# The score product of a spiking recommender as two float32r passes, with the table fetched 14 chunks ahead and statistics in groups of two steps

## The chip, the cores and the metric

The kernel runs on one NeuronCore of a Trainium2 chip. The metric is device time in microseconds (us) of one execution; several runs give a median. Engines are called by their names: TensorE (PE in the profile, its weight loads PEld), VectorE (DVE), ScalarE (ACT), GpSimd (POOL) and SyncE (SP, which here only issues transfers). The 16 DMA engines of the core carry all transfers.

## What is computed

The inputs are a batch of 1,024 sequences of 50 item numbers, a length for each sequence, a table of 100,001 items with 128 float32 features, and gamma and beta of a batch normalisation. Cut to what matters:

```python
emb = emb_table.at[0].set(0.0)
prefix = jnp.cumsum(emb[seq], axis=1)
denom = jnp.minimum(t_idx[None, :], lengths[:, None])
uF = prefix / denom[:, :, None]
y = (uF - uF.mean(axis=0)) * rsqrt(uF.var(axis=0) + 1e-5) * gamma + beta
# for each of the 50 steps: v += (x - v) / 2; spike = v >= 1; v -= spike
rate = spikes.mean(axis=0)          # 1024 x 128
scores = rate @ emb.T               # 1024 x 100001
```

The scores alone are 409.6 MB in float32, and the table is 51.2 MB.

## The kernel before

There are two stages, and features lie on the 128 partitions in both.

**First stage, the steps (lines 59 to 149).** For each of the 50 time steps, GpSimd issues eight indirect gathers (line 105), 128 rows of the table each, into a buffer `e` of which there are six. ScalarE clears a buffer before its gathers (line 103). TensorE transposes the eight blocks into a PSUM tile `eT` (line 115). VectorE adds it to the running prefix `pre` (line 116), divides by the lengths into `uF` (117) and takes batch statistics (120, 121). Five steps form a group (TG = 5): only when the statistics of all five stand are the short operations on mean and variance done (124 to 136). Then ScalarE normalises each step into `xh` (141, 143), and VectorE runs the neuron: `v`, `negv` and `count` (146 to 148), three passes over 128x1024 a step. At the end `rateT`, the count divided by 50, is the stationary side of the score product (149).

**Second stage, the scores (lines 163 to 203).** The table is taken in 49 chunks of 2,048 items, the last one shorter. A chunk is fetched by a transfer of 1 MB that ScalarE issues, into one of three `rows` buffers (166 to 173). TensorE transposes it, in 16 blocks, into two PSUM tiles `pt` of 1,024 columns (183). VectorE and ScalarE in turn copy them to `embT` (186, by the helper of lines 155 to 161). For each of eight blocks of 128 sequences TensorE multiplies: four products of 512 columns, into two PSUM tiles `po` of 1,024 columns (195). VectorE evicts the first and ScalarE the second into an output tile `o` (202), and SyncE issues the store of 1 MB (203). There are eight `o` buffers and four PSUM tiles, shared by `eT`, `pt` and `po`.

A scheduler sets the order of the instructions on each engine from the program, and may move an instruction of the second stage ahead of late ones of the first. Each engine then works through its list in that order, and waits at an instruction until all that it needs is there.

Of the kernel before, what the change touches and what calls it, by code (L numbers as in the profile page):

```python
# [12 lines left out]
F32 = mybir.dt.float32  # L13
I32 = mybir.dt.int32
# [14 lines left out]
def rec_kernel(  # L29
# [19 lines left out]
    rowp = ctx.enter_context(tc.tile_pool(name="rows", bufs=3))  # L49
    embp = ctx.enter_context(tc.tile_pool(name="embT", bufs=2))  # L50
# [4 lines left out]
    # rateT[d, b]: the mean of the spikes over time, the stationary side of the score product.  # L55
    rateT = const.tile([P, B], F32, tag="rateT", name="rateT")

    # ---------------- prefix means, batch norm and spikes: D on partitions, batch on columns
    with ExitStack() as ph:
# [6 lines left out]
        # Item 0 has a zero embedding: its index goes out of bounds, where the gather leaves the  # L66
        # zeros that the tile was cleared to.
# [8 lines left out]
        # 1 / min(t, length) = max(1 / t, 1 / length)  # L76
# [9 lines left out]
        # x / tau with tau = 2: half of gamma and beta.  # L86
# [8 lines left out]
        nc.vector.memset(count, 0.0)  # L95

        for g in range(T // TG):
# [25 lines left out]
            # rsqrt(var + eps): a square root, its reciprocal, and one Newton step on that.  # L123
# [14 lines left out]
            for j in range(TG):  # L138
# [5 lines left out]
                # v <- v + (x - v) / 2; spike = v >= V_TH; v <- v - spike, kept negated.  # L144
# [10 lines left out]
    def evacuate(dst, src):  # L155
        nonlocal turn
        if turn % 2 == 0:
            nc.vector.tensor_copy(dst, src)  # L158
        else:
            nc.scalar.copy(dst, src)  # L160
        turn += 1

    for c0 in range(0, N, CH):
        w = min(CH, N - c0)
        full, rest = divmod(w, P)
        rows = rowp.tile([P, CH // P, D], F32, tag="rows", name=f"rows_{c0}")
        if full:
            nc.scalar.dma_start(
                out=rows[:, :full, :],
                in_=table[c0 : c0 + full * P, :].rearrange("(k p) d -> p k d", p=P),  # L170
            )
# [51 lines left out]
```

## Time and profile before

| | |
|---|---|
| median of 3 runs | 2107.3 us (2107.03 to 2107.64) |
| the profiled execution: its span, first to last instruction | 2106.9 us |
| TensorE busy, matmuls | 1627.1 us, 77% |
| VectorE busy | 912.5 us, 43% |
| ScalarE busy | 609.2 us, 29% |
| GpSimd busy | 457.0 us, 22% |
| HBM written, read | 409.60 MB, 78.15 MB |

The profile is of one execution, and its span is what there is of that execution's own time; it stands 0.4 us under the median. Shares of the span are averages over two stages that work differently, so a reader should go by stretches: the first stage ends at the first product of the scores, 640.28 us after the start, and the second takes the rest. Busy time of a matmul is counted from its start to its modelled end, and neighbours overlap; how far apart they follow each other is read from a run of many, divided by their number.

### The profile page before, as it was taken

The page shows a single profiled execution, that of the slowest core. Times are in us where ns is not written, and L with a number is a line of the kernel's source. Part 1 is how long each engine was busy: PE and PEld are TensorE (multiplying, and loading weights), DVE is VectorE, ACT ScalarE, POOL GpSimd, SP SyncE. Part 2 cuts the span into 40 slices and gives each one's busy share as a digit, 9 for nine tenths or more (in the row PEclk, how much of TensorE's full clock was granted, in tenths as well). Part 3 has the DMA queues.
Part 4 walks back from the last instruction along what each step waited for, and adds up shares of the span by engine and source line. Part 5 has one row for each costly group of instructions (what it writes and reads, how often), then busy time and mean ns, then how long its engine had stood idle before and what let it go on. Part 6 is the DMA issues. An engine that isn't in the chain of part 4 may idle for free.

```text
span 2106.9 us, 13798 instructions
## 1 busy us (share of the span) xinstructions
PE 1627.1 (77%) x4318; PEld 754.1 (36%) x4318; DVE 912.5 (43%) x921; ACT 609.2 (29%) x651; POOL 457.0 (22%) x406
## 2 busy tenths in 40 slices
PE   2333233333318999999999999999999999999998
PEld 1111111111103444444444444444444444444444
DVE  4443766557574333333333333333333333333333
ACT  2212323323132323333333323332333333323332
POOL 6777777777700000000000000000000000000000
PEclk9999999999999999999999999999999999999999
DMA  4111111111105888887888788888887888788867
GB/s 116 48 45 47 43 46 46 46 45 44 44 25 222 313 320 317 317 311 315 319 319 312 315 317 316 316 316 317 317 316 310 317 319 319 309 316 317 313 277 292
DMA packets 97862, 488.69 MB, mean 232 GB/s; under 512 B 14811, under 2 KB 16508, under 8 KB 48636
## 3 DMA queue, kind: packets, MB, share of 16 engines
q1 hardware_dynamic: 57920, 410.36, 48.6%
q10 hardware_dynamic: 27068, 51.20, 8.2%
q0 software_dynamic: 12800, 26.24, 4.7%
q8 instruction: 34, 0.56, 0.1%
q14 instruction: 40, 0.33, 0.0%
HBM read 78.15 MB, written 409.60 MB: 232 GB/s over the span
## 4 chain that ended last, share of the span: by engine, by line
PE 66%; issue 14%; POOL 13%; DVE 5%; DMA 1%; POOLq 0%; ACT 0%; ACTq 0%
PE po L195 64%; POOL e L105 13%; DVE embT L158 3%; PE pt L183 2%; DMA e<-in_L_rec_emb_table,idx 1%; DVE v L146 1%; DVE negv L147 1%; POOLq L105 0%; DVE bs L120 0%; DVE uF L117 0%; DVE pre L116 0%; DVE count L148 0%; ACT xh L143 0%; ACT uF L141 0%; POOLq L219 0%
## 5 line engine op out<-in xcount | busy, mean ns | idle before, releaser
L195 PE MATMUL po<-embT,rateT 128*128 128x512 f32 x3136 | 1356.1, 593 | 71.0 <-DVE rateT L149 49.5
L195 PEld LDWEIGHTS po<-embT,rateT 128*128 128x128 f32 x3136 | 591.8, 190 | 807.0 <-issue 655.9
L158 DVE COPY o<-po 128x1024 f32<-128x1024 f32 x392 | 480.0, 1224 | 859.8 <-PE po L195 859.8
L160 ACT COPY o<-po 128x1024 f32<-128x1024 f32 (+1 forms) x392 | 394.4, 1006 | 995.3 <-PE po L195 995.3
L115 PE MATMUL eT<-ident,e 128*128 128x128 f32 x400 | 183.6, 469 | 402.2 <-DMA e<-in_L_rec_emb_table,idx 355.5
L105 POOL DMA_INDIRECT e<-in_L_rec_emb_table,idx x400 | 456.3, 1141 | 126.1 <-issue 114.9
L115 PEld LDWEIGHTS eT<-ident,e 128*128 128x128 f32 x400 | 72.5, 184 | 513.0 <-DMA e<-in_L_rec_emb_table,idx 399.9
L103 ACT ACTIVATE e<-e 128x1024 uint32<-128x1024 uint32 x50 | 52.3, 1055 | 368.2 <-PE eT L115 263.2
L158 DVE COPY embT<-pt 128x1024 f32<-128x1024 f32 x49 | 60.0, 1225 | 93.5 <-PE pt L183 93.5
L183 PEld LDWEIGHTS pt<-ident,rows 128*128 128x128 f32 x782 | 90.0, 142 | 27.2 <-issue 25.5
L183 PE MATMUL pt<-ident,rows 128*128 128x128 f32 x782 | 95.4, 276 | 1.3 <-DVE embT L158 1.3
L116 DVE TENSOR_TENSOR pre<-pre,eT 128x1024 f32<-128x1024 f32 x50 | 59.7, 1195 | 65.6 <-issue 39.6
L146 DVE SCALAR_TENSOR_TENSOR v<-negv,xh 128x1024 f32<-128x1024 f32 x50 | 61.1, 1221 | 55.5 <-issue 40.2
L143 ACT ACTIVATE xh<-uF,hgb,a 128x1024 f32<-128x1024 f32 x50 | 59.9, 1228 | 62.2 <-DVE a L134 32.3
L120 DVE BATCH_NORM_STATS2 bs<-uF 128x6 f32<-128x512 f32 x100 | 66.5, 685 | 0.5
L117 DVE SCALAR_TENSOR_TENSOR uF<-rlen,pre 128x1024 f32<-128x1024 f32 x50 | 61.0, 1219 | 0.4
L148 DVE SCALAR_TENSOR_TENSOR count<-v,count 128x1024 f32<-128x1024 f32 x50 | 61.0, 1219 | 0.0
L147 DVE SCALAR_TENSOR_TENSOR negv<-v 128x1024 f32<-128x1024 f32 x50 | 60.7, 1214 | 0.2
L160 ACT COPY embT<-pt 128x1024 f32<-128x1024 f32 (+1 forms) x49 | 49.3, 1006 | 33.0 <-PE pt L183 33.0
L141 ACT ACTIVATE uF<-uF,nm 128x1024 f32<-128x1024 f32 x50 | 53.2, 1133 | 0.0
L128 DVE RECIPROCAL r<-r 128x5 f32<-128x5 f32 x10 | 1.9, 189 | 110.3 <-issue 80.8
L127 ACT ACTIVATE r<-ve 128x5 f32<-128x5 f32 x10 | 2.0, 196 | 33.7 <-DVE ve L125 33.7
(26 smaller groups left out, 37.1 us busy)
## 6 DMA issues: line engine op xcount, KB each, us to landing
scores<-o SPq DMA_DIRECT2D x384, 1024.0 KB, 3.9
scores<-o SPq DMA_DIRECT2D x8, 848.5 KB, 3.5
e<-in_L_rec_emb_table,idx POOLq DMA_INDIRECT x400
rows<-in_L_rec_emb_table ACTq DMA_DIRECT2D x1, 832.0 KB, 7.2
rows<-in_L_rec_emb_table ACTq DMA_DIRECT2D x48, 0.5 KB, 7.7
len_i<-in_r_lengths SPq DMA_DIRECT2D x1, 512.0 KB, 5.2
seq_sb<-in_r_seq SPq DMA_DIRECT2D x1, 200.0 KB, 2.9
rows<-in_L_rec_emb_table ACTq DMA_DIRECT2D x1, 16.5 KB
```

Source lines behind the costliest of these rows:

```text
L105: nc.gpsimd.indirect_dma_start(out=e[:, n * P : (n + 1) * P], out_offset=None, in_=table, in_offset=bass.IndirectOffsetOnAxis(ap=idx[:, n, ...
L115: nc.tensor.transpose(eT[:, n * P : (n + 1) * P], e[:, n * P : (n + 1) * P], ident)
L117: nc.vector.scalar_tensor_tensor(uF[:, j, :], rlen, 1.0 / (t + 1), pre, ALU.max, ALU.mult)
L120: nc.vector.bn_stats(bs[:, h, :], uF[:, j, h * BANK : (h + 1) * BANK])
L143: nc.scalar.activation(xh, x, AF.Identity, bias=hgb[:, 1:2], scale=a[:, j : j + 1])
L146: nc.vector.scalar_tensor_tensor(v, negv, -0.5, xh, ALU.mult, ALU.add)
L147: nc.vector.scalar_tensor_tensor(negv, v, V_TH, v, ALU.is_ge, ALU.subtract)
L148: nc.vector.scalar_tensor_tensor(count, v, V_TH, count, ALU.is_ge, ALU.add)
L158: nc.vector.tensor_copy(dst, src)
L160: nc.scalar.copy(dst, src)
L183: nc.tensor.transpose(pt[:, k0 : k0 + kw], rows[:kw, (h0 + k0) // P, :], ident[:kw, :kw])
L195: nc.tensor.matmul(po[:, k0 : k0 + kw], lhsT=rateT[:, n * P : (n + 1) * P], rhs=embT[:, h0 + k0 : h0 + k0 + kw], start=True, stop=True,)
```

## The change

1. **The score product.** `rateT` gives way to `countR`, the integer counts themselves, in the type float32r. Each half of a chunk leaves PSUM in two parts: `hi`, which ScalarE writes as float32r, and `lo`, the difference between the PSUM tile and `hi`, which VectorE computes and writes as float32r. Each float32 product of 512 columns becomes two float32r products that add up in PSUM, one with `hi` and one with `lo`. The division by 50 is done at the eviction, as a multiplication by VectorE and ScalarE in turn.
2. **The table.** There are 14 `rows` buffers instead of three. The fetches go out from SyncE instead of ScalarE: 14 ahead of the first step, and each further one when the transposes of a chunk are through, in SyncE's list between the stores of two chunks.
3. **The steps.** TG = 2: the statistics are finished for two steps together, in 25 groups instead of 10.
4. **The buffers.** There are four `o` buffers instead of eight.

```diff
-TG = 5  # time steps whose batch statistics are finished together
+TG = 2
+AHEAD = 14
...
-    rowp = ctx.enter_context(tc.tile_pool(name="rows", bufs=3))
-    embp = ctx.enter_context(tc.tile_pool(name="embT", bufs=2))
+    rowp = ctx.enter_context(tc.tile_pool(name="rows", bufs=AHEAD))
...
-    rateT = const.tile([P, B], F32, tag="rateT", name="rateT")
+    countR = const.tile([P, B], F32R, tag="countR", name="countR")
+    held = {}
+    def fetch(c0):
+        w = min(CH, N - c0)
+        full, rest = divmod(w, P)
+        rows = rowp.tile([P, CH // P, D], F32, tag="rows", name=f"rows_{c0}")
+        if full:
+            nc.sync.dma_start(
+                out=rows[:, :full, :],
+                in_=table[c0 : c0 + full * P, :].rearrange("(k p) d -> p k d", p=P),
+            )
...
+        held[c0] = rows
+    def rows_of(c0):
+        if c0 + AHEAD * CH < N:
+            todo.append(c0 + AHEAD * CH)
+        return held.pop(c0)
...
+        for c0 in range(0, min(AHEAD * CH, N), CH):
+            fetch(c0)
 
         for g in range(T // TG):
...
-        nc.vector.tensor_scalar_mul(rateT, count, 1.0 / T)
-    op = ctx.enter_context(tc.tile_pool(name="o", bufs=8))
+        nc.vector.tensor_copy(countR, count)
+    op = ctx.enter_context(tc.tile_pool(name="o", bufs=4))
+    embp = ctx.enter_context(tc.tile_pool(name="embT", bufs=2))
...
-            nc.scalar.dma_start(
-                out=rows[:, :full, :],
...
+        rows = rows_of(c0)
+        hi = embp.tile([P, CH], F32R, tag="hi", name=f"hi_{c0}")
+        lo = embp.tile([P, CH], F32R, tag="lo", name=f"lo_{c0}")
...
-            evacuate(embT[:, h0 : h0 + hw], pt[:, :hw])
+            nc.scalar.copy(hi[:, h0 : h0 + hw], pt[:, :hw])
+            nc.vector.tensor_tensor(
+                lo[:, h0 : h0 + hw], pt[:, :hw], hi[:, h0 : h0 + hw].bitcast(F32), ALU.subtract
+            )
+        while todo:
+            fetch(todo.pop())
...
-                    nc.tensor.matmul(
-                        po[:, k0 : k0 + kw],
-                        lhsT=rateT[:, n * P : (n + 1) * P],
-                        rhs=embT[:, h0 + k0 : h0 + k0 + kw],
-                        start=True,
-                        stop=True,
-                    )
-                evacuate(o[:, h0 : h0 + hw], po[:, :hw])
+                    kw += kw % 2
+                    for part, first in ((hi, True), (lo, False)):
+                        nc.tensor.matmul(
+                            po[:, k0 : k0 + kw],
+                            lhsT=countR[:, n * P : (n + 1) * P],
+                            rhs=part[:, h0 + k0 : h0 + k0 + kw],
+                            start=first,
+                            stop=not first,
+                        )
+                if turn % 2 == 0:
+                    nc.vector.tensor_scalar_mul(o[:, h0 : h0 + hw], po[:, :hw], 1.0 / T)
+                else:
+                    nc.scalar.mul(o[:, h0 : h0 + hw], po[:, :hw], 1.0 / T)
+                turn += 1
```

The scheduler's order changes at three places that the prediction speaks of.

**VectorE, late in the first stage.** Before, this stood in VectorE's list (`embT` and `pt` are the first chunk's copy and its transposes; `eT`, `pre`, `uF` are of steps 46 and 47, counted from 0, and `v` is of step 40):

```order
L116 TENSOR_TENSOR pre<-pre,eT_2474 128x1024
L131 SCALAR_TENSOR_TENSOR q_2362<-q_2362,ve_2357 128x5
L121 BN_AGGR mv_2406<-bs_2444 128x2
L117 SCALAR_TENSOR_TENSOR uF_2405<-rlen,pre 128x1024
L132 SCALAR_TENSOR_TENSOR r_2359<-q_2362,r_2359 128x5
L158 COPY embT_2672<-pt_0_2673 128x1024
L134 TENSOR_SCALAR a_2366<-r_2359,hgb 128x5
L120 BN_STATS bs_2485<-uF_2405 128x6 x2
L116 TENSOR_TENSOR pre<-pre,eT_2515 128x1024
L146 SCALAR_TENSOR_TENSOR v_2373<-negv,xh_2371 128x1024
```

With the change the list ends the first stage so (`v_2900` and `v_2907` are the last two steps, `lo` is the first chunk's):

```order
L175 SCALAR_TENSOR_TENSOR v_2900<-negv,xh_2898 128x1024
L176 SCALAR_TENSOR_TENSOR negv<-v_2900 128x1024
L177 SCALAR_TENSOR_TENSOR count<-v_2900,count 128x1024
L175 SCALAR_TENSOR_TENSOR v_2907<-negv,xh_2905 128x1024
L205 TENSOR_TENSOR lo_2924<-pt_0_2925,hi_2923 128x1024
L176 SCALAR_TENSOR_TENSOR negv<-v_2907 128x1024
L177 SCALAR_TENSOR_TENSOR count<-v_2907,count 128x1024
L205 TENSOR_TENSOR lo_2924<-pt_1024_2936,hi_2923 128x1024
L178 CAST countR<-count 128x1024
L228 TENSOR_SCALAR o_0_2949<-po_0_0_2950 128x1024
```

The first chunk's copy out of `pt` stood ahead of the statistics of step 46, of steps 47 to 49, and of the neuron of steps 40 to 49; now its successor, the subtraction into `lo`, stands among the neuron's last passes. In TensorE's list the first chunk's transposes follow those of all 50 steps, before and now.

**SyncE, at the start.** Before, SyncE's list went on from the four small loads to the first store:

```order
L84 DMA gb<-in_L_rec_gamma 128x1
L85 DMA gb<-in_L_rec_beta 128x1
L203 DMA scores<-o_0_2693 128x2048
L203 DMA scores<-o_1_2703 128x2048
L203 DMA scores<-o_2_2713 128x2048
```

and now the 14 fetches stand between (the `rows` are those of chunks 0 to 13, of which five are shown):

```order
L110 DMA gb<-in_L_rec_gamma 128x1
L111 DMA gb<-in_L_rec_beta 128x1
L67 DMA rows_107<-in_L_rec_emb_table 128x16x128
L67 DMA rows_110<-in_L_rec_emb_table 128x16x128
L67 DMA rows_112<-in_L_rec_emb_table 128x16x128
L67 DMA rows_114<-in_L_rec_emb_table 128x16x128
L67 DMA rows_116<-in_L_rec_emb_table 128x16x128
```

The fetch of chunk 14 stands ahead of the first store, and each later one ahead of the first store of a chunk. In GpSimd's list nothing is moved: eight gathers for each step, and from the ninth on each waits for the landing of the gather eight places ahead of it.

**VectorE, between two chunks.** Now the list reads, from the sixth block of a chunk to the first of the next:

```order
L228 TENSOR_SCALAR o_5_3019<-po_5_0_3020 128x1024
L228 TENSOR_SCALAR o_6_3033<-po_6_0_3034 128x1024
L205 TENSOR_TENSOR lo_3062<-pt_0_3063,hi_3061 128x1024
L228 TENSOR_SCALAR o_7_3047<-po_7_0_3048 128x1024
L205 TENSOR_TENSOR lo_3062<-pt_1024_3074,hi_3061 128x1024
L228 TENSOR_SCALAR o_0_3087<-po_0_0_3088 128x1024
```

and before:

```order
L158 COPY o_5_2743<-po_5_0_2744 128x1024
L158 COPY o_6_2753<-po_6_0_2754 128x1024
L158 COPY o_7_2763<-po_7_0_2764 128x1024
L158 COPY embT_2775<-pt_0_2776 128x1024
L158 COPY o_0_2796<-po_0_0_2797 128x1024
```

The first half of the next chunk (`lo_3062<-pt_0`) is subtracted ahead of the eviction of the last block (`o_7`), where before the one copy stood behind it. TensorE's list holds, now as before, the 16 transposes of the next chunk behind the last product of this one.

## Rows read from the trace of the kernel before

**Rows 1.** The page, span in 40 equal slices: TensorE, GpSimd, DMA, busy tenths

```profile
PE   2333233333318999999999999999999999999998
...
POOL 6777777777700000000000000000000000000000
...
DMA  4111111111105888887888788888887888788867
```

**Rows 2.** The page, costliest groups: line, engine, operation; busy us, mean ns; idle

```profile
L195 PE MATMUL po<-embT,rateT 128*128 128x512 f32 x3136 | 1356.1, 593 | 71.0 <-DVE rateT L149 49.5
...
L158 DVE COPY o<-po 128x1024 f32<-128x1024 f32 x392 | 480.0, 1224 | 859.8 <-PE po L195 859.8
...
L160 ACT COPY o<-po 128x1024 f32<-128x1024 f32 (+1 forms) x392 | 394.4, 1006 | 995.3 <-PE po L195 995.3
...
L105 POOL DMA_INDIRECT e<-in_L_rec_emb_table,idx x400 | 456.3, 1141 | 126.1 <-issue 114.9
...
L146 DVE SCALAR_TENSOR_TENSOR v<-negv,xh 128x1024 f32<-128x1024 f32 x50 | 61.1, 1221 | 55.5 <-issue 40.2
...
L120 DVE BATCH_NORM_STATS2 bs<-uF 128x6 f32<-128x512 f32 x100 | 66.5, 685 | 0.5
```

**Rows 3.** Chain that ended last, one chunk: start us, us, what

```profile
670.79 1.24 DVE embT L158
...
672.07 27.73 PE po L195 x64
...
700.72 1.24 DVE embT L158
```

**Rows 4.** Busy time in four stretches: engines, granted clock, DMA share, GB/s

```profile
556.90:587.50 30.60, 12.09 (x30) 5.60 (x30) 0.03 (x1) 0.00 (x0) 20.71 (x21) 1.00 0.18 46
...
1000.00:1300.00 300.00, 295.56 (x808) 139.43 (x806) 110.96 (x91) 91.24 (x101) 0.00 (x0) 1.00 0.82 315
...
1001.00:1011.00 10.00, 9.76 (x23) 4.48 (x24) 3.45 (x4) 2.87 (x3) 0.00 (x0) 1.00 1.01 347
...
1013.00:1032.00 19.00, 18.56 (x56) 9.07 (x55) 7.35 (x6) 6.07 (x7) 0.00 (x0) 1.00 0.74 304
```

**Rows 5.** The page, DMA queues, and the stores' time from issue to landing

```profile
q1 hardware_dynamic: 57920, 410.36, 48.6%
q10 hardware_dynamic: 27068, 51.20, 8.2%
...
scores<-o SPq DMA_DIRECT2D x384, 1024.0 KB, 3.9
```

**Rows 6.** Timeline, end of first stage: start us, us, engine, what, idle before, releaser

```profile
582.71 1.00 POOL L105 DMA_INDIRECT e<-in_L_rec_emb_table,idx  x1 [0.30 <-issue]
...
585.29 0.47 PE L115 MATMUL eT<-ident,e 128*128 128x128 f32 x1 [0.75 <-DMA e<-in_L_rec_emb_table,idx]
...
587.50 1.22 DVE L158 COPY embT<-pt 128x1024 f32<-128x1024 f32 x1 [30.58 <-PE pt L183]
...
621.76 1.23 DVE L146 SCALAR_TENSOR_TENSOR v<-negv,xh 128x1024 f32<-128x1024 f32 x1 [2.15 <-ACT xh L143]
...
640.28 1.22 PE L195 MATMUL po<-embT,rateT 128*128 128x512 f32 x1 [49.53 <-DVE rateT L149]
```

**Rows 7.** Timeline, a table fetch and gathers near it

```profile
18.64 0.69 ACTq L168 DMA_DIRECT2D rows<-in_L_rec_emb_table  x1
...
20.64 1.24 POOL L105 DMA_INDIRECT e<-in_L_rec_emb_table,idx  x1 [0.30 <-issue]
...
24.98 0.90 PE L115 MATMUL eT<-ident,e 128*128 128x128 f32 x3 [3.84 <-DMA e<-in_L_rec_emb_table,idx]
```

**Rows 8.** Timeline, the 16 transposes of a chunk and their weight loads

```profile
998.89 1.91 PE L183 MATMUL pt<-ident,rows 128*128 128x128 f32 x16
998.89 1.67 PEld L183 LDWEIGHTS pt<-ident,rows 128*128 128x128 f32 x15 [0.29 <-issue]
```

More of the change, by code (lines that the diff above doesn't have):

```diff
@@ L13 @@
 F32 = mybir.dt.float32
+F32R = mybir.dt.float32r
 I32 = mybir.dt.int32
@@ L48, in rec_kernel @@
     psum = ctx.enter_context(tc.tile_pool(name="psum", bufs=4, space=bass.MemoryType.PSUM))
-    rowp = ctx.enter_context(tc.tile_pool(name="rows", bufs=3))
-    embp = ctx.enter_context(tc.tile_pool(name="embT", bufs=2))
+    rowp = ctx.enter_context(tc.tile_pool(name="rows", bufs=AHEAD))
     ident = const.tile([P, P], F32, tag="ident", name="ident")
     make_identity(nc, ident)
-    rateT = const.tile([P, B], F32, tag="rateT", name="rateT")
+    countR = const.tile([P, B], F32R, tag="countR", name="countR")
[9 more added lines that the diff above has]
+            )
+        if rest:
+            nc.sync.dma_start(out=rows[:rest, full, :], in_=table[c0 + full * P : c0 + w, :])
+        if c0 == 0:
+            nc.vector.memset(rows[0:1, 0, :], 0.0)
+        held[c0] = rows
[3 more added lines that the diff above has]
+        return held.pop(c0)
+    todo = []
     with ExitStack() as ph:
@@ L148, in rec_kernel @@
                 nc.vector.scalar_tensor_tensor(count, v, V_TH, count, ALU.is_ge, ALU.add)
-        nc.vector.tensor_scalar_mul(rateT, count, 1.0 / T)
-    op = ctx.enter_context(tc.tile_pool(name="o", bufs=8))
+        nc.vector.tensor_copy(countR, count)
+    op = ctx.enter_context(tc.tile_pool(name="o", bufs=4))
+    embp = ctx.enter_context(tc.tile_pool(name="embT", bufs=2))
     turn = 0
[L155 to L161, printed above, removed]
     for c0 in range(0, N, CH):
         w = min(CH, N - c0)
-        full, rest = divmod(w, P)
-        rows = rowp.tile([P, CH // P, D], F32, tag="rows", name=f"rows_{c0}")
-        if full:
-            nc.scalar.dma_start(
-                out=rows[:, :full, :],
-                in_=table[c0 : c0 + full * P, :].rearrange("(k p) d -> p k d", p=P),
-            )
-        if rest:
-            nc.scalar.dma_start(out=rows[:rest, full, :], in_=table[c0 + full * P : c0 + w, :])
-        if c0 == 0:
-            nc.vector.memset(rows[0:1, 0, :], 0.0)
-        embT = embp.tile([P, CH], F32, tag="embT", name=f"embT_{c0}")
+        we = w + w % 2
+        rows = rows_of(c0)
+        hi = embp.tile([P, CH], F32R, tag="hi", name=f"hi_{c0}")
+        lo = embp.tile([P, CH], F32R, tag="lo", name=f"lo_{c0}")
+        if we > w:
+            nc.vector.memset(hi[:, w:we].bitcast(F32), 0.0)
+            nc.vector.memset(lo[:, w:we].bitcast(F32), 0.0)
         for h0 in range(0, w, HALF):
@@ L194, in rec_kernel @@
                     kw = min(BANK, hw - k0)
-                    nc.tensor.matmul(
-                        po[:, k0 : k0 + kw],
-                        lhsT=rateT[:, n * P : (n + 1) * P],
-                        rhs=embT[:, h0 + k0 : h0 + k0 + kw],
-                        start=True,
-                        stop=True,
-                    )
-                evacuate(o[:, h0 : h0 + hw], po[:, :hw])
+                    kw += kw % 2
[12 more added lines that the diff above has]
+                turn += 1
             nc.sync.dma_start(out=out[n * P : (n + 1) * P, c0 : c0 + w], in_=o[:, :w])
```

## The prediction

> **What bounds the kernel now.** I read the slices first, to part the stages [rows 1]. In the first eleven GpSimd is the busiest, at seven tenths; in the last 27 TensorE is at nine or more and DMA at about eight. Then the groups [rows 2]: the products of line 195 lead, and VectorE's and ScalarE's evictions of `o` wait for them. The chain shows what a chunk is made of [rows 3]: 27.73 us of products, 64 instructions, so 0.433 us each, and 29.93 us from one chunk's `embT` copy to the next; the other 2.2 us are transposes, the first copy and hand-overs. So the second stage is bound by TensorE, at a granted clock of 1.00, that is 2.4 GHz [rows 4]. The reader should see how little room DMA has beside it: 0.82 of it is busy [rows 4]. A change that only makes the products cheaper runs into that, and so the sum is made of the transfers, not of the products.
>
> The first stage is set by GpSimd's gathers: 400 of them at 1.141 us [rows 2] and 0.30 us between two [rows 6]. Its last gather ends at 583.7, and the last transposes of `e` at 585.8 [rows 6]. But the first product starts only at 640.3. Between these lies a fault of the order: VectorE waits 30.58 us for the first chunk's `pt` [rows 6], because the `embT` copy stands in its list ahead of work on the steps, while `pt` is transposed after all gathers. In those 30.6 us VectorE does 0.03 us of work [rows 4].
>
> **The change, part by part.**
>
> *The tail of the first stage.* With the change the copy's successor `lo` stands at the very end of the neuron, so the stall goes. What is late next is VectorE's own chain behind the last gather. From its list I count 16 full passes (`pre`, `uF`, six of each of the last two groups, two `lo`) at 1.22 us [rows 2], 19.5 us; two half statistics at 0.685 [rows 2], 1.4 us; and 3 us for short operations and the wait for ScalarE's `xh`, which was 2.15 us in the last group before [rows 6]. That is 24 us where 54.5 passed before (585.8 to 640.3). GpSimd pays a little: while VectorE stood still its gathers took 1.00 us [rows 6], against a mean of 1.14 [rows 2], and 21 were issued in the stall [rows 4]: 3 us. The 15 additional groups' short operations lie beside the gathers; uncovered, 15 times the 3 us above would cost 45 us, but VectorE is far from full there.
>
> *Fourteen fetches ahead.* They are queued in front of the gathers. A gather issued at 20.64, behind one fetch issued at 18.64, was used only at 24.98, when three landed together [rows 7], 3.1 us after its issue had ended. So a gather waits for a fetch already handed over, some 3 us. GpSimd may be eight gathers ahead, eight times 1.30 us, or 10.4 us, which covers that. I take 3 us for the start. Ends: nothing, or the rival below. The first stage then ends at 585.8 + 24 + 3 + 3 = **616 us**.
>
> *The products.* Each float32 product ran as two instructions of 0.433 us, at two cycles a column; that is 0.866 us. Now there are two float32r instructions per product, so the count stays at 64 a chunk. No row has a float32r product. Its price lies between nothing and 0.433. Four cycles a column fit operands taken in two halves, four partial products; and the code's own split says that a float32r operand holds one part only. So I take one cycle, a quarter of 0.866: 0.217 us, 13.9 us a chunk. As a price that only a page states: the Trainium skill (FP8 and Floating Point Precision, TensorE Precision Notes) gives four passes for true FP32, by which one pass is also an estimated 0.217 us and the sum the same.
>
> *Between two chunks* TensorE idles longer. Eight transposes take 0.95 us (16 in 1.91 [rows 8]), `hi` 1.01 on ScalarE, `lo` 1.22 on VectorE, and then VectorE evicts half of `o_7`, 1.22, before the tile for `po_0` is free [rows 2]: with hand-overs 4.6 us. TensorE's chunk is 13.9 + 4.6 = 18.5 us. VectorE has ten passes of 1.22, ScalarE ten of 1.01: 12.2 and 10.1 us.
>
> *The transfers.* A chunk now takes 0.82 of 29.93, which is 24.5 us of DMA work [rows 3, 4]. Where stores run alone DMA is 0.74 busy at 304 GB/s, so 411 GB/s while busy [rows 4]; the 8.39 MB of a chunk's stores are 20.4 us, and a fetch accounts for 4.1. This is above TensorE's 18.5 with and without a fetch: **DMA becomes the bound.** In chunks of 2,048 there are 48.83; 14 are fetched ahead and need 20.4 us, 34.83 need 24.5: 286 + 853 = 1,139 us. The queues agree: 48.6% and 8.2% of the span [rows 5] are 1,197 us, 24.5 for each of 48.83 chunks. In a stretch with a fetch and stores queued the share was already 1.01 [rows 4], so the engines can be full; I add 2% for joins: 1,163 us. Ends: all 446 MB at 411 GB/s, 1,085 us; all at the 315 GB/s of the stage now, 1,416 us [rows 4].
>
> *Four output tiles.* They must cover the gap between chunks. A store of 1.05 MB is 2.55 us of work. When `o_2` has landed and `o_6` is evicted, three stores are queued, and with `o_6` and `o_7` there are 11.8 us of work. `o_0` of the next chunk follows after `o_6` (1.2), transposes, `hi`, `lo`, half of `o_7`, the second `lo`, four products and an eviction: about 9 us. So the queue does not run dry, by some 2 us. Without that cover each us of gap costs 49 us. Fetches in SyncE's list hold up nothing: their wait, for the chunk's transposes, ends before the stores behind them are ready.
>
> *The ends.* Before the first store stand four products and an eviction, 4 us; after the last, its landing, 3.
>
> **The sum.** 616 + 4 + 1,163 + 3 = **1,786 us**, against the profiled execution's 2,106.9, which stands 0.4 us under the median of 2,107.3. A difference of 0.2%, 4 us, is what a measurement of this kernel can tell.
>
> **The rivals.**
> 1. *The gathers starve at the start.* If the 14 fetches all go before a gather's packets, they take 14 times 4.1, 57 us; GpSimd stops after its first eight gathers, and the first stage grows by some 45 us: 1,831 us. For it speaks that the gathers landed only when the fetch was through [rows 7]; against it, that SyncE hands over fetches one by one, and the gathers get in between.
> 2. *Weight loads come into the open.* Each product loads its weights. At 0.433 us that was hidden; if a load of 0.11 us (15 in 1.67 [rows 8]) now stands before each product, a chunk is 64 times 0.328 plus 4.6, 25.6 us, and TensorE binds again: 616 + 1,250 + 7 = 1,873 us. Against it, 16 transposes with loads of their own follow each other every 0.12 us [rows 8]. The Trainium skill (TensorE: Matmul & The Clock Gate, What overlaps and what doesn't, in the part on packing small matmuls) has loads overlap products only in another row group; by that rule this rival would hold, and the transposes' trace disagrees.
> 3. *The memory side binds below a full queue.* If 315 GB/s is all that is sustained, the stage is 1,416 us, the total 2,039. Against it, stretches at 411 GB/s while busy, and idle DMA. The Trainium skill (Perfetto Trace Analysis, Engine Utilization) puts a core's memory bandwidth at 358 GB/s; by that the stage would be an estimated 1,246 us and the total 1,869, and the busy stretches of this trace go above it.
> 4. *Slower: float32r costs as much as a float32 instruction.* At 0.433 us a chunk's products stay at 27.7 us, and the longer gap comes on top: 32.3 us, times 48.83, 1,577 us; the total is 2,200. From 0.30 us a product on, TensorE binds again; from 0.40 on, the kernel is slower than before. For it speaks that the row nearest in kind is 0.433, and that both move four bytes an element; against it, the four cycles a column.
>
> **How the numbers follow.** The forecast has 0.60, within 1,740 to 1,835; the starved start 0.12; the weight loads, or gaps of 2 us between chunks, which come to the same, 0.10; the memory side 0.09, anywhere up to its 2,039; the full price 0.08; a price near 0.40 us, at which nothing is won or lost, 0.01. The range of 1,740 to 1,920 leaves out the full price, the balance, the slower half of the memory rival and the edges of the forecast, some 2 in 10. Faster by over 0.2% is 0.91, slower 0.08, the same 0.01.
>
> **What would show it.** In the changed kernel's profile DMA should stand at nine tenths or more through the second stage, near 385 GB/s; VectorE and ScalarE should wait for stores ahead of `o`; products should follow each other every 0.22 us with waits between; the first product should start near 616 us, and no wait of VectorE near 30 us should be left. A product at 0.33 or 0.43, DMA below nine tenths, or GpSimd idle in the first 60 us would make the prediction wrong, each in its own way.

## The result, and the profile after

The changed kernel takes 1,760.0 us, the median of four runs (1,758.76 to 1,761.08), against 2,107.45 for the kernel before, measured beside it. The ratio is 0.835, with a 95% interval of 0.834 to 0.836: faster by 16.5%. The forecast was 1,786.0, 28.4 us more than the profiled execution's span of 1,757.6 and 1.5% over the median. The direction and the bound were right. Two terms were off, and they partly cancel: against the forecast the first stage ended 9 us later, and the second was 38 us shorter.

The page, the span in 40 equal slices (TensorE, GpSimd, DMA, in tenths), and the queue of the stores with its issues:

```profile
PE   2333223223222268777778778787777788888886
...
POOL 6777777778878500000000000000000000000000
...
DMA  9611111111111269999999999999999999999998
...
q1 hardware_dynamic: 84988, 461.56, 67.4%
...
scores<-o SPq DMA_DIRECT2D x384, 1024.0 KB, 9.0
```

The nine has moved from TensorE's row to that of DMA [rows 1]. Stores and fetches are now one queue, and a store lands 9.0 us after its issue where it was 3.9 [rows 5]: it stands in line. The page's costliest groups (busy us, mean ns, then the idle time before them and what ended most of it):

```profile
L220 PE MATMUL po<-hi,countR 128*128 128x512 f32 x1568 | 652.6, 421 | 228.1 <-ACT o L230 136.5
L228 DVE TENSOR_SCALAR o<-po 128x1024 f32<-128x1024 f32 x392 | 475.4, 1221 | 437.6 <-DMA scores<-o 404.2
...
L230 ACT ACTIVATE o<-po 128x1024 f32<-128x1024 f32 (+1 forms) x392 | 396.0, 1023 | 581.3 <-DMA scores<-o 394.1
L134 POOL DMA_INDIRECT e<-in_L_rec_emb_table,idx x400 | 472.5, 1181 | 126.1 <-issue 117.9
```

Before, both evictions of `o` waited for TensorE's `po` [rows 2]. Now they wait for stores, some 400 us each: there is no free output tile until one has landed. TensorE in turn waits for ScalarE's eviction. That is the bound seen from the engines. In the windows (us; busy us and instructions of PE, PEld, DVE, ACT, POOL; granted clock; DMA share; GB/s) it is seen directly, in the stretch with fetches and in the one after the last:

```profile
700.00:1000.00 300.00, 235.11 (x992) 181.74 (x991) 147.04 (x125) 122.96 (x125) 0.00 (x0) 0.93 1.01 395
...
1430.00:1700.00 270.00, 230.47 (x1031) 172.20 (x1031) 152.46 (x129) 127.17 (x128) 0.00 (x0) 0.99 0.98 403
```

From 0.82 and 315 GB/s [rows 4] to 1.01 and 395. Later fetches are issued at 647.42, and, 33 chunks on, at 1,438.66: 23.98 us a chunk. What a chunk without a fetch takes is read from the transposes of chunks 35 and 47, behind the last fetch:

```profile
1456.53 1.97 PE L201 MATMUL pt<-ident,rows 128*128 128x128 f32 x16 [0.49 <-ACT o L230]
...
1707.05 1.97 PE L201 MATMUL pt<-ident,rows 128*128 128x128 f32 x16 [0.70 <-ACT o L230]
```

That is 12 chunks in 250.52 us, 20.9 us each.

The border of a chunk, in the timeline:

```profile
1001.17 1.91 PE L201 MATMUL pt<-ident,rows 128*128 128x128 f32 x16
...
1002.24 1.93 ACT L204 CAST hi<-pt 128x1024 fp32r<-128x1024 f32 x2 [1.33 <-PE pt L201]
1003.28 1.22 DVE L205 TENSOR_TENSOR lo<-pt,hi 128x1024 fp32r<-128x1024 f32 x1 [2.16 <-ACT hi L204]
...
1004.42 1.22 DVE L228 TENSOR_SCALAR o<-po 128x1024 f32<-128x1024 f32 x1
...
1004.56 0.50 PE L220 MATMUL po<-hi,countR 128*128 128x512 f32 x1 [1.49 <-DVE lo L205]
...
1009.00 0.39 PE L220 MATMUL po<-hi,countR 128*128 128x512 f32 x1
1009.00 0.19 PEld L220 LDWEIGHTS po<-lo,countR 128*128 128x128 f32 x1
1009.23 0.39 PE L220 MATMUL po<-lo,countR 128*128 128x512 f32 x1
```

Products start 0.23 us apart, and the 0.19 us load of the next one lies under the running one. From the transposes' start to the next product pass 3.4 us, not 4.6: the product starts as `lo` ends, while VectorE's eviction of `o_7`, begun at 1,004.42, still runs. It does not wait for that eviction, here or at any of the other 47 borders, which take 3.39 to 3.46 us.

The end of the first stage, in the timeline:

```profile
598.87 0.99 POOL L134 DMA_INDIRECT e<-in_L_rec_emb_table,idx  x1 [0.30 <-issue]
...
601.39 0.47 PE L144 MATMUL eT<-ident,e 128*128 128x128 f32 x1 [0.70 <-DMA e<-in_L_rec_emb_table,idx]
...
624.37 0.69 DVE L178 CAST countR<-count 128x1024 fp32r<-128x1024 f32 x1
...
625.21 0.77 PE L220 MATMUL po<-hi,countR 128*128 128x512 f32 x1 [19.93 <-DVE countR L178]
```

The last gather ends at 599.9 where it ended at 583.7 [rows 6], so 16 us later; the tail behind the last transposes is 23.3 us where it was 54.5.

### The profile page after: what moved, and what is told of

It is laid out like the page before. It is cut to its first block, busy times and chain, and to the rows that moved or that the text cites. A ratio compares the mean times of both kernels' runs of the same rounds, so it can differ in the third digit from the quotient of the medians.

```text
span 1757.6 us, 13866 instructions
## 1 busy us (share of the span) xinstructions
PE 1084.4 (62%) x4318; PEld 765.1 (44%) x4318; DVE 959.1 (55%) x1077; ACT 653.6 (37%) x667; POOL 473.2 (27%) x406
## 3 DMA queue, kind: packets, MB, share of 16 engines
q1 hardware_dynamic: 84988, 461.56, 67.4%
## 4 chain that ended last, share of the span: by engine, by line
DMA 45%; POOL 16%; issue 16%; PE 13%; DVE 6%; ACT 3%; POOLq 0%; SPq 0%; DVEq 0%; ACTq 0%
DMA scores<-o 42%; POOL e L134 16%; PE po L220 11%; DVE o L228 3%; DMA e<-in_L_rec_emb_table,idx 2%; ACT o L230 2%; ACT hi L204 1%; PE pt L201 1%; DVE lo L205 1%; POOLq L134 0%; SPq L232 0%; DVE v L175 0%; DVE negv L176 0%; DVE count L177 0%; DVEq L228 0%
## 5 line engine op out<-in xcount | busy, mean ns | idle before, releaser
L220 PE MATMUL po<-hi,countR 128*128 128x512 f32 x1568 | 652.6, 421 | 228.1 <-ACT o L230 136.5
L228 DVE TENSOR_SCALAR o<-po 128x1024 f32<-128x1024 f32 x392 | 475.4, 1221 | 437.6 <-DMA scores<-o 404.2
L220 PE MATMUL po<-lo,countR 128*128 128x512 f32 x1568 | 641.1, 412 | 0.0
L230 ACT ACTIVATE o<-po 128x1024 f32<-128x1024 f32 (+1 forms) x392 | 396.0, 1023 | 581.3 <-DMA scores<-o 394.1
L134 POOL DMA_INDIRECT e<-in_L_rec_emb_table,idx x400 | 472.5, 1181 | 126.1 <-issue 117.9
L220 PEld LDWEIGHTS po<-hi,countR 128*128 128x128 f32 x1568 | 312.4, 199 | 352.4 <-ACT o L230 181.8
L144 PE MATMUL eT<-ident,e 128*128 128x128 f32 x400 | 177.7, 467 | 424.2 <-DMA e<-in_L_rec_emb_table,idx 345.6
L220 PEld LDWEIGHTS po<-lo,countR 128*128 128x128 f32 x1568 | 312.8, 199 | 76.4 <-DVE lo L205 16.0
L205 DVE TENSOR_TENSOR lo<-pt,hi 128x1024 fp32r<-128x1024 f32 x98 | 119.2, 1216 | 106.7 <-ACT hi L204 106.7
L204 ACT CAST hi<-pt 128x1024 fp32r<-128x1024 f32 x98 | 94.1, 1012 | 66.7 <-PE pt L201 66.7
## 6 DMA issues: line engine op xcount, KB each, us to landing
rows<-in_L_rec_emb_table SPq DMA_DIRECT2D x1, 16.5 KB
```

What stands on the lines that cost most here:

```text
L134: nc.gpsimd.indirect_dma_start(out=e[:, n * P : (n + 1) * P], out_offset=None, in_=table, in_offset=bass.IndirectOffsetOnAxis(ap=idx[:, n, ...
L144: nc.tensor.transpose(eT[:, n * P : (n + 1) * P], e[:, n * P : (n + 1) * P], ident)
L204: nc.scalar.copy(hi[:, h0 : h0 + hw], pt[:, :hw])
L205: nc.vector.tensor_tensor(lo[:, h0 : h0 + hw], pt[:, :hw], hi[:, h0 : h0 + hw].bitcast(F32), ALU.subtract)
L220: nc.tensor.matmul(po[:, k0 : k0 + kw], lhsT=countR[:, n * P : (n + 1) * P], rhs=part[:, h0 + k0 : h0 + k0 + kw], start=first, stop=not first,
L228: nc.vector.tensor_scalar_mul(o[:, h0 : h0 + hw], po[:, :hw], 1.0 / T)
```

## The experiments

All twelve are given with the ratio to the kernel before, measured on the same chip. That kernel took 2,107 to 2,116 us there, so runs on different chips are compared by their ratios. Diffs of all but the first are against the changed kernel.

**1. Groups of two alone.** The kernel before, with

```diff
-TG = 5
+TG = 2
```

> The kernel before with one edit, groups of two steps. Theory (the transfers bind the second stage of the changed kernel; the first stage gains only its tail): the first chunk's copy moves behind the last step's statistics in VectorE's list, the 30.6 us wait goes, the first product starts at 625 us as in the changed kernel and not at 640, the second stage stays at 1,467 us: 2,092 us. Rival (grouping by two costs what the wait gave, through slower gathers): 2,105 us or more.

2,100.49 us, ratio 0.995 (0.994 to 0.997). The first product moves from 640.3 to 632.9 us, and the wait of 30.6 us for `pt` is gone: the copy now stands late in VectorE's list, at 614.3. But the last gather ends at 602.5, 19 us later than before, at a mean of 1.19 us. The time lies between the two expectations. The order was a fault, as the prediction said, but mending it by groups of two gives back most of its worth in slower gathers. How much of that comes from the lost stall and how much from the groups, run 1 can't part; runs 11 and 12 do.

**2. The product in float32.** One copy `hi` by ScalarE in float32, no `lo`, one float32 product; fetches, groups and tiles as changed.

```diff
-                    for part, first in ((hi, True), (lo, False)):
+                    for part, first in ((hi, True),):
...
-                            stop=not first,
+                            stop=True,
```

(and `hi`, `countR` of type float32, the subtraction left out)

> The changed kernel with float32 products again: one copy of each half chunk by ScalarE, no lo, one float32 product instead of two float32r ones; fetches, groups and buffers as changed. Theory: TensorE binds the second stage again, 48.83 chunks of 29.9 us, 1,460 us, so 2,085 to 2,095 us in all; so nearly the whole gain hangs on the products. Rival (the fetch ahead and the groups brought the gain): below 1,900 us.

2,109.55 us, ratio 1.000 (0.998 to 1.002): nothing is left of the gain. A chunk takes some 29.8 us, and DMA falls back to 0.82 and 317 GB/s (same columns as the windows above):

```profile
700.00:1000.00 300.00, 296.81 (x807) 139.72 (x806) 99.09 (x81) 100.05 (x100) 0.00 (x0) 1.00 0.82 317
```

So the rest of the change, as it stands, is worth nothing without the cheaper product. It also brought the old fault back on another engine. Waits, from 560 to 645 us (us in total, times, longest):

```profile
ACT hi L202 <- PE pt L199: 40.1, 2, 38.0
...
DVE r L157 <- ACT r L156: 29.9, 1, 29.9
```

Here ScalarE's first `hi` stands ahead of work on the steps, and waits 38 us; the first product starts at 642.7, 17 us later than in the changed kernel, which accounts for a time some 15 us above the expected 2,085 to 2,095.

**3. `hi` alone.** The second product, with `lo`, is left out, so the scores lack the low part.

```diff
-                    for part, first in ((hi, True), (lo, False)):
+                    for part, first in ((hi, True),):
...
-                            stop=not first,
+                            stop=True,
```

> The changed kernel without the product with lo (lo is still computed and not used, so the scores hold the hi part alone): 32 products a chunk instead of 64. Theory: the transfers bind, and 7.3 us less of TensorE a chunk change nothing: 1,755 to 1,762 us. Rival (TensorE's products, its slow stretches or the gap between chunks are still on the path): 7.3 us times 48.83 is 356 us, and any good part of that: below 1,700 us.

1,758.44 us, ratio 0.832 (0.829 to 0.835), the changed kernel's own time, with half its products. The window from 700 to 1000:

```profile
700.00:1000.00 300.00, 187.88 (x616) 122.11 (x614) 150.61 (x127) 127.41 (x127) 0.00 (x0) 0.78 1.02 395
```

The share stays at 1.02 and 395 GB/s, the chunk at 23.9 us. TensorE has ample room in the changed kernel, and the transfers bind.

**4. Half the stores.** Of each output tile only the first half is stored, so half the scores are left unwritten; all engines do the same work.

```diff
-            nc.sync.dma_start(out=out[n * P : (n + 1) * P, c0 : c0 + w], in_=o[:, :w])
+            nc.sync.dma_start(out=out[n * P : (n + 1) * P, c0 : c0 + w // 2], in_=o[:, : w // 2])
```

> The changed kernel storing only the first half of each output tile's columns, so the other half of the scores is left unwritten: 205 MB of stores instead of 410. Theory: the transfers fall to some 14 us a chunk and TensorE with its gap binds at 64 times 0.227 plus 4.6, 19.1 us a chunk: 625 + 935 + 7, about 1,567 us. Rival (something other than the transfers sets 24 us a chunk): 1,700 us or more.

1,504.33 us, ratio 0.713 (0.710 to 0.715). Now TensorE is the bound, at 0.96 of the stretch (same columns as the windows above):

```profile
700.00:1000.00 300.00, 287.44 (x1360) 233.17 (x1359) 204.99 (x170) 170.42 (x171) 0.00 (x0) 1.00 0.81 297
```

From the first product at 633.4 to the end of the span at 1,501.1 a chunk takes 17.8 us. With 64 products at 0.227 us (14.5) that leaves 3.3 us that are not products, of which 2.2 lie between the start of the transposes and the next product. The expectation had 19.1 us a chunk, and the time came out 63 us below it. The second stage has 1,132.4 − 867.7 = 265 us between what the engines need and what the transfers take.

**5. Three fetches ahead.**

```diff
-AHEAD = 14
+AHEAD = 3
```

> The changed kernel with three chunks fetched ahead instead of 14. Theory (transfers bind, and a fetch in the second stage costs what the period of a chunk shows, 23.98 us with a fetch against 21.27 without): 11 more fetches of 2.7 us, some 30 us more: 1,785 to 1,800 us. Rival (fetches are hidden in the second stage anyway): 1,760 us.

1,804.35 us, ratio 0.853 (0.850 to 0.855). The second stage has 11 more fetches and is 1,166.6 us, 34.2 longer: 3.1 us a fetch. The 2.7 expected was too low because the 21.27 us taken for a chunk without a fetch also held stores that were still queued; 20.9, from the transposes, gives 3.1. The first product came at 637.6, 12 us later than in the changed kernel's profile. Of that 3 us are slower gathers (475.8 us in all, against 472.5), and 9 us are a single pause of ScalarE:

```profile
185.68 1.06 ACT L132 ACTIVATE e<-e 128x1024 uint32<-128x1024 uint32 x1 [17.15 <-remote]
...
187.01 0.99 POOL L134 DMA_INDIRECT e<-in_L_rec_emb_table,idx  x1 [9.27 <-ACT e L132]
```

The profiles of runs 3 to 9 each hold such a pause of GpSimd, once or twice, of 2 to 9 us; those of the kernel before, the changed kernel and runs 1, 2, 10, 11 and 12 hold none. What causes it is not shown.

**6. All fetches from ScalarE.**

```diff
-            nc.sync.dma_start(
+            nc.scalar.dma_start(
                 out=rows[:, :full, :],
```

> The changed kernel with the table's fetches issued by ScalarE, as before, instead of SyncE. Theory (the 16 DMA engines are full either way): the same within 5 us. Rival (a fetch in the queue of the stores is cheaper than one that mixes with them from a queue of its own, and that is why a fetch cost less than the 4.1 us I had worked out): each of 35 fetches 1.4 us dearer, 1,800 to 1,810 us. A third: ScalarE's issue waits in its list behind evictions that wait for stores, and fetches come late: also slower.

1,795.08 us, ratio 0.849 (0.847 to 0.851): slower than the changed kernel, but with a faster second stage, which none of the three expectations had. Waits in the first 80 us, and the window from 700 to 1000:

```profile
PE eT L144 <- DMA e<-in_L_rec_emb_table,idx: 71.4, 17, 57.3
...
POOL e L134 <- ACT e L132: 51.2, 1, 51.2
...
700.00:1000.00 300.00, 237.72 (x1048) 177.15 (x1048) 155.21 (x130) 129.80 (x144) 0.00 (x0) 0.98 1.02 409
```

The 14 issues stand in ScalarE's list ahead of its clearing of `e`; GpSimd waits 51.2 us for that, and the first product starts at 687.7. A starved start like that of the prediction's first rival is real here, but it comes through an engine's list: the issues follow each other some 3.6 us apart, and the clearing waits behind all of them. In the changed kernel SyncE's first ten issues take 37 us too, but no step waits behind them. The second surprise is the rate: 409 GB/s where the changed kernel has 395, at the same share.

**7. Eight output tiles, 10 fetches ahead** (all fetches from SyncE again, and 10 of them ahead, to make room for the tiles).

```diff
-AHEAD = 14
+AHEAD = 10
...
-    op = ctx.enter_context(tc.tile_pool(name="o", bufs=4))
+    op = ctx.enter_context(tc.tile_pool(name="o", bufs=8))
```

> The changed kernel with eight output tiles instead of four, and ten chunks fetched ahead instead of 14 to make room. Theory (four tiles cover the gap between chunks): only the four fetches show, 1,768 to 1,775 us. Rival (the queue runs dry between chunks, as the share of 0.98 in the last 15 chunks hints): eight tiles give back up to 0.8 us a chunk, 40 us, and the time falls to 1,730 to 1,755 us.

1,777.57 us, ratio 0.840 (0.837 to 0.843). This is 3 us above the range of the theory. With fetches a chunk is 23.95 us by the transposes of chunks 5 to 33 (23.97 with four tiles), so four tiles do cover the border. The second stage is 11.2 us longer with four more fetches, 2.8 us each, near the 3.1 of run 5.

**8. Longer runs of the table.** A partition takes 16 neighbouring items, 8 KB at a stretch, instead of 16 pieces of 512 bytes; `hi` and `lo` are then written with a stride of 16 elements.

```diff
-                in_=table[c0 : c0 + full * P, :].rearrange("(k p) d -> p k d", p=P),
+                in_=table[c0 : c0 + full * P, :].rearrange("(p k) d -> p k d" if full == CH // P else "(k p) d -> p k d", p=P),
...
+                hv = hi.rearrange("d (p k) -> d k p", k=CH // P)[:, kb : kb + k8, :]
+                lv = lo.rearrange("d (p k) -> d k p", k=CH // P)[:, kb : kb + k8, :]
+                pv = pt.rearrange("d (k p) -> d k p", p=P)
+                nc.scalar.copy(hv, pv)
+                nc.vector.tensor_tensor(lv, pv, hv.bitcast(F32), ALU.subtract)
...
```

> The changed kernel with each partition fetching 16 neighbouring items, 8 KB in one run instead of 16 runs of 512 bytes; hi and lo are written with a stride of 16 to put the items in order again. Theory (transfers bind, so cheaper transfers are time): a fetch at the stores' 411 GB/s is 2.55 us of DMA work instead of 2.7 to 4.1: 5 to 50 us less, 1,710 to 1,755 us, if the strided writes of hi and lo cost no more. Rival (the strided writes lengthen the gap between chunks): 1,760 us or more.

1,809.52 us, ratio 0.855 (0.851 to 0.858). The queue's time falls from 1,185 us (67.4% of 1,757.6) to 1,147 (63.5% of 1,806.7), but the strided writes are dear. The queue, and groups of the stretch from 1000 to 1300 (busy us, mean ns):

```profile
q1 hardware_dynamic: 66556, 461.56, 63.5%
...
L211 DVE TENSOR_TENSOR lo<-pt,hi 128x1024 fp32r<-128x1024 f32 x24 | 45.7, 1905 | 43.7 <-ACT hi L210 43.7
L210 ACT CAST hi<-pt 128x1024 fp32r<-128x1024 f32 x24 | 43.1, 1894 | 17.9 <-PE pt L201 17.9
```

1.9 us each instead of 1.2 and 1.0, all of it at the border of the chunk. A chunk takes 23.9 us with a fetch and without one, and DMA is at 0.87 in the last chunks: there the border binds, not the transfers. The gain in the transfers is lost to it, as the rival had it.

**9. A queue for each.** The first 15 fetches from SyncE, the later ones from ScalarE.

```diff
     def fetch(c0):
+        eng = nc.sync if c0 <= AHEAD * CH else nc.scalar
...
-            nc.sync.dma_start(
+            eng.dma_start(
```

> The changed kernel, but only the first 15 fetches go out from SyncE; the fetches of chunks 15 to 48 go out from ScalarE, so that in the second stage stores and fetches have a queue each. Theory A (a separate queue is what made the second stage of the run with all fetches on ScalarE faster, 23.0 us a chunk against 23.98): the first stage stays where the changed kernel has it, 625 to 640 us, the second falls by some 34 us, to about 1,098; total 1,725 to 1,740 us. Rival B (that stage was faster for another reason, its late start or the few chunks left; the memory gives 394 GB/s however it is asked): 1,755 to 1,765 us, share 1.01 at 394 GB/s as before.

1,742.15 us, ratio 0.823 (0.822 to 0.825), faster than the changed kernel. The window from 700 to 1000, and the two queues:

```profile
700.00:1000.00 300.00, 233.16 (x1040) 172.39 (x1040) 155.48 (x130) 129.21 (x145) 0.00 (x0) 1.00 1.02 411
...
q1 hardware_dynamic: 65840, 426.09, 60.7%
q10 hardware_dynamic: 19148, 35.47, 6.0%
```

A chunk takes 23.1 us with a fetch, 20.8 without, and the second stage 1,103.8, 29 less. The same 461.56 MB now take 66.7% of 1,738.5 us, 1,160 us of the queues' time, where they took 1,185 in one queue. The first product came at 634.7, 9 us later than in the changed kernel's profile, 6 of them a pause as in run 5, and the total lies 2 us above the range expected. Theory A holds for the second stage: the separate queue is worth about 0.9 us for each chunk with a fetch. The Trainium skill (DMA: Bandwidth & Descriptors, Rules for kernel authors) says that spreading transfers over issuing engines does not raise bandwidth; here it does, from 395 to 411 GB/s. In the packets both sides gain: between 700 and 1300 us a store's 8 KB packet takes 317 ns on average instead of 326, a fetch's 2 KB packet 96 instead of 103. Why was not tried, and stays open.

**10. A queue for each, and eight tiles** (with 10 fetches ahead: the edits of runs 7 and 9 together).

> As the one with split queues, with eight output tiles and 10 fetches ahead. Theory A (a chunk with a fetch is held by the transfers alone, so more tiles give nothing there; only the chunks without a fetch, where the share was 0.98, gain, 21.3 to 20.5 us): 38.8 chunks of 23.0 and 10 of 20.5, 1,098 us, the same as with four tiles and 14 ahead, total within 10 us of that run. Rival B (four tiles do leave the queue dry between chunks): faster than that run by more than 15 us.

1,745.67 us, ratio 0.825 (0.823 to 0.827), 3.5 us from run 9, as Theory A had it, but in part by luck. The second stage is 1,112.2 us, not the 1,098 of the theory and 8.4 longer than in run 9: it has four more fetches. A chunk with a fetch is 23.09 us by the transposes of chunks 5 to 33, against 23.13 there. What made the total the same is a first product at 625.4, 9.3 us earlier than in run 9's profile, 6 of them because there was no pause of ScalarE. Rival B falls all the same: eight tiles do not shorten the stage.

**11. Groups of five, eight tiles** (run 7, and)

```diff
-TG = 2
+TG = 5
```

> The changed kernel with eight output tiles, 10 fetches ahead and groups of five steps (groups of two measured 1,777.6 us beside these buffers). Theory A (small groups shorten the tail behind the last gather: with five, 15 passes of the neuron at 1.22 us, not six, can stand behind it, 11 us): first product 7 to 11 us later than with groups of two, total 1,785 to 1,789. Rival B (the grouping costs as much in gathers slowed by VectorE's passes as it saves in the tail): within 4 us of 1,777.6. If the stall of 30 us came back with groups of five, 1,805 or more.

1,770.37 us, ratio 0.837 (0.835 to 0.839): not later than run 7 but 7 us earlier, though the intervals of the ratios touch. Both theories missed. The tail behind the last transposes does grow, from 21.6 to 26.7 us (609.98 to 631.61 there, 592.53 to 619.22 here), but the last gather ends 17 us sooner: the gathers cost 13 us less (463.1 against 476.3), and 4 us are a pause that run 7's profile has and this one has not. The stall did not come back: VectorE's longest wait from 500 us to the end of the stage is 6.7 us. So that the stall stays away does not hang on groups of two, once `hi` and `lo` have changed the lists.

**12. All that helped** (the edits of runs 7, 9 and 11 together).

> Both gains together: a queue each for stores and for later fetches, eight output tiles, 10 fetches ahead, and groups of five steps instead of two. Theory A (the two act in different stages and add up): the second stage as in the run with split queues and eight tiles, 1,104 to 1,112 us, the first product near 620 as in the run with groups of five, gathers near 1.16 us; total 1,733 to 1,740 us, some 7 under that run's 1,745.7. Rival B (the earlier end with groups of five was one execution's luck in when gathers and passes meet): within 4 us of 1,745.7, gathers at 1.18 us or more.

1,732.74 us (1,731.58 to 1,733.83), ratio 0.822 (0.821 to 0.824): the lowest median, and 1.6% under the changed kernel by the ratios, though its interval overlaps those of runs 9 and 10, and the kernel before was 7 us faster beside it than beside run 10 (2,107.88 against 2,114.8). By the time alone the gain over run 10 is not clear. By the profiles Theory A holds, and the two gains add up: a second stage of 1,111.7 us and a first product at 618.1, where run 10 has 1,112.2 and 625.4. The gathers of run 10 (groups of two), and of this run (groups of five), by the page:

```profile
L135 POOL DMA_INDIRECT e<-in_L_rec_emb_table,idx x400 | 474.3, 1186 | 126.1 <-issue 116.1
```

```profile
L135 POOL DMA_INDIRECT e<-in_L_rec_emb_table,idx x400 | 462.0, 1155 | 126.1 <-issue 110.9
```

The 12.3 us between them is the whole of what the last gather ends earlier (588.35 against 600.66, start); 5 us of it go to the longer tail.

## Why the prediction came out as it did

**What bounds.** Right. The sum was made of transfers, and DMA reads 1.01 in the chunks with a fetch and 0.98 behind them; half the products left out change nothing (run 3), half the stores left out give 256 us (run 4).

**The products.** Right, and the term on which the gain hangs (run 2). Taken were 0.217 us, measured 0.227: the estimate of "one cycle, a quarter of 0.866" was 4% short, and it does not matter under the transfers. Rival 4, at 0.433, fell: products stand 0.23 us apart at a granted clock of 1.00, and 0.43 where it was at half, as below. The four passes that the Trainium skill (FP8 and Floating Point Precision, TensorE Precision Notes) gives for true FP32 fit: 0.866 against 0.227 is a ratio of 3.8.

**The border of a chunk.** Mis-sized, without effect: 3.4 us, not 4.6. The step that failed is "and then VectorE evicts half of `o_7`, 1.22, before the tile for `po_0` is free"; the timeline shows the product starting beside that eviction. TensorE's chunk is 17.8 us where it binds (run 4), not 18.5.

**The transfers.** This is the term that was off by most: taken 4 + 1,163 + 3 = 1,170 us, measured 1,132.4. The step that failed is "I add 2% for joins", 24 us in the sum (2% of 1,139 is 23). In the chunks with a fetch the share leaves no room for them: it reads 1.01 and not 0.98. Only the last chunks, at 0.98, took that much more than their price, some 7 us in all. The other 14 us are in the split of a chunk. Taken were 24.5 us with a fetch and 20.4 without; measured were 24.0 and 20.9, and one fetch fewer falls into the stage, since chunk 14's is issued at 605.37. So a fetch costs 3.1 us by the difference, as by run 5, not the 4.1 that came from setting one stretch's share against another's. The shares of the queues [rows 5] come nearer: 48.6% of the span is 21.0 us a chunk for the stores, and 8.2% is 3.5 for a fetch.

Rival 3 fell with this: 315 GB/s was what the old kernel asked for, not what the memory gives, and the 10 us at a share of 1.01 and 347 GB/s [rows 4] were too short to price by: over 300 us the full queue reads 395. The estimate for it from the Trainium skill (Perfetto Trace Analysis, Engine Utilization), 358 GB/s, lies below what this core kept up for a millisecond, 395. That section gives 358 as a core's share when both cores of a pair are at work, and for one alone some 120% of it, an estimated 430 GB/s; no stretch of 300 us here went above 414.

**Four output tiles.** Right in effect, by runs 7 and 10: eight tiles shorten a chunk by 0.02 to 0.04 us.

**The start.** Right that the fetches do not starve the gathers. In the first 70 us DMA reads 0.96, and GpSimd issues its gathers between, most of them every 1.30 us; its idle time over all 400 is 126.1 us, now as before. Rival 1 at 1,831 fell; run 6 shows a starved start that comes about in another way.

**The end of the first stage.** 616 was forecast and 625.2 measured. The tail is right: 23.3 us for 24. The step that failed is "GpSimd pays a little ... 3 us". The gathers cost 472.5 − 456.3 = 16.2 us more; the 3 us for the start were not needed. I counted only the 21 gathers beside the old stall, and took it that the other passes would slow the gathers as before. With groups of five and no stall the gathers cost 463.1 and 462.0 us (runs 11 and 12), 6 to 7 more than before, so even that part was short. The other 10 us come with the groups of two: beside otherwise equal kernels, 476.3 us in run 7 and 474.3 in run 10. I had priced the groups only by their short operations. Timeline of the changed kernel, GpSimd and VectorE:

```profile
298.39 1.22 DVE L145 TENSOR_TENSOR pre<-pre,eT 128x1024 f32<-128x1024 f32 x1
299.13 0.99 POOL L134 DMA_INDIRECT e<-in_L_rec_emb_table,idx  x1 [0.30 <-issue]
...
299.71 1.17 DVE L146 SCALAR_TENSOR_TENSOR uF<-rlen,pre 128x1024 f32<-128x1024 f32 x1
300.43 1.31 POOL L134 DMA_INDIRECT e<-in_L_rec_emb_table,idx  x1 [0.30 <-issue]
...
305.58 1.22 DVE L176 SCALAR_TENSOR_TENSOR negv<-v 128x1024 f32<-128x1024 f32 x1
305.63 2.03 POOL L134 DMA_INDIRECT e<-in_L_rec_emb_table,idx  x1 [0.30 <-issue]
306.72 1.22 DVE L177 SCALAR_TENSOR_TENSOR count<-v,count 128x1024 f32<-128x1024 f32 x1
307.85 1.22 DVE L175 SCALAR_TENSOR_TENSOR v<-negv,xh 128x1024 f32<-128x1024 f32 x1
307.97 1.97 POOL L134 DMA_INDIRECT e<-in_L_rec_emb_table,idx  x1 [0.31 <-issue]
...
312.85 1.00 POOL L134 DMA_INDIRECT e<-in_L_rec_emb_table,idx  x1 [0.30 <-issue]
```

What counts is the pass in which a gather starts. The one at 299.13 starts in `pre` and takes 0.99 us. Those at 300.43, 305.63 and 307.97 start in `uF`, `negv` and `v`, and each ends 0.87 us after that pass does. It is the same for all 400, sorted by the pass that runs 0.1 us after a gather's start. There are 94 of 1.05 us or more, and 93 of them start in `uF`, `v`, `negv` or `count`, passes whose two inputs both lie in SBUF; every one ends 0.86 to 0.88 us after that pass. Of the 79 that start in `pre`, one input of which lies in PSUM, or in the statistics, which have one input, none takes over 1.00 us. In every other run, too, no gather that starts there takes over 1.01.

The excess of the 94 over 1.00 us is 73.7 us, 0.78 each. Before it was 57.5 us for 97 gathers, and with groups of five (run 11) 64.3 for 107, 0.60 each. So with groups of two the number of gathers that wait does not grow, but they start nearer to the beginning of a pass; why they fall so was not tried. Groups of two, expected to be worth up to 11 us in the tail, save 5 there and cost 12 (runs 10 and 12).

**Weight loads.** Rival 2 fell. A load of 0.19 us is longer than the 0.11 that I took for it from the transposes, and would have cost 64 × 0.19 = 12 us a chunk in the open; products 0.227 us apart leave no room for it between them. Loads do run under products here, though the rule cited for that rival (the Trainium skill, TensorE: Matmul & The Clock Gate, What overlaps and what doesn't) wants another row group.

## What to carry to other kernels

When an engine is made faster, make the sum for what binds next, and take its price from rows in which that resource was full; a margin for joins that no row shows was here the largest single miss. A fault in the order of one engine's list can be cover for another engine: before counting the whole wait as a gain, ask who ran undisturbed in it. Before passes are regrouped, ask which of them another engine has to wait for; here these were VectorE's passes with both inputs in SBUF, and GpSimd's gathers waited. And try a queue each for large stores and large loads, worth 0.9 us a chunk here, but keep early issues off a list on which the first steps wait.

## What the runs showed of the hardware that was not expected

- A separate queue for the fetches raised the rate at the same share, 408 to 414 GB/s against 393 to 397 between 700 and 1300 us (runs 6, 9, 10 and 12 against the changed kernel and runs 3, 5, 7 and 11).
- A gather of GpSimd that starts in one of VectorE's passes with two inputs in SBUF lasts until 0.87 us after that pass, up to 2.04 us in all; one that starts in a pass with an input in PSUM, or with a single input, takes 1.00 us (93 and 79 gathers of the changed kernel, as above). The Trainium skill (SBUF — State Buffer, SBUF: two separate sides) has VectorE and GpSimd share a pair of ports, for which a VectorE operation with two SBUF inputs makes a GpSimd operation that reads SBUF wait until it is through; the trace agrees, on either side of that condition.
- TensorE's clock falls in the transfer-bound stage, at no cost that the time shows. The timeline, and the window from 1020 to 1023, in which the granted clock was 0.50, that is 1.2 GHz:

```profile
1016.24 0.39 PE L220 MATMUL po<-lo,countR 128*128 128x512 f32 x1
1020.03 0.79 PE L220 MATMUL po<-hi,countR 128*128 128x512 f32 x1 [3.40 <-ACT o L230]
1020.62 0.63 PE L220 MATMUL po<-lo,countR 128*128 128x512 f32 x1
...
1023.16 0.39 PE L220 MATMUL po<-lo,countR 128*128 128x512 f32 x1
1023.39 0.39 PE L220 MATMUL po<-hi,countR 128*128 128x512 f32 x1
```

```profile
1020.00:1023.00 3.00, 2.97 (x7) 2.39 (x8) 1.42 (x2) 1.02 (x1) 0.00 (x0) 0.50 1.00 415
```

TensorE had stood idle for 3.40 us, waiting for ScalarE's eviction and so for a store; its products then follow each other every 0.43 us and from 1,023.16 on every 0.23 again. With `hi` alone (run 3) the mean clock of the stage was 0.76 to 0.78, and the time the same.
